# A selective-scan kernel on one core: the first column of `u B` made on GpSimd and copied in ahead of the product, Silu blocks opened for copies, and other buffers

## The chip, the cores and the metric

The kernel runs on one core of a Trainium2 chip. The metric is the device time of one execution in microseconds (us); less is better. Engine names are those of the profile: PE is TensorE's matmul, PEld its weight load, DVE is VectorE, ACT is ScalarE, POOL is GpSimd, SP is SyncE, which issues most DMAs.

## The reference, cut to what matters

The input has 4 images of 256 channels and 64 x 64 positions. Two mixers follow each other on every position, and then a layer of 8 experts with 1 choice per token. The change lies in the first mixer, a Mamba block with 512 inner channels and 16 states:

```
dt = softplus(dbl[..., :DT_RANK] @ dt_w.T + dt_b)
A = -exp(A_log)
def step(h, inp):
    dt_l, B_l, C_l, x_l = inp
    dA = exp(dt_l[..., None] * A)
    h = dA * h + (dt_l * x_l)[..., None] * B_l[:, None, :]
    y = einsum('bdn,bn->bd', h, C_l)
    return (h, y)
```

The second mixer (a state space block with 8 heads) is computed in matrix form, chunk by chunk, in `ssd`. All arithmetic is float32.

## The kernel before, in words

The program has three phases one after the other: `mixers`, `experts` and `turn`. The change touches only `mixers`, which takes the first five sixths of the time.

**Chunks and stages.** The positions of each image are cut into 16 chunks of `T` = 256, 64 chunks in all. A chunk goes through `front0` (projections and convolution of the first mixer), `mid0` (dt, and `u` = dt times x, written to DRAM), `scan`, `tail0`, `front1`, and two chunks later through `ssd` and `back1`. At any time, stages of several chunks are under way side by side.

**The scan.** `scan` works in 16 units per chunk: `j` (0 to 3) takes 128 of the 512 channels, `f` (0 to 3) takes four of the 16 states. Partitions hold 4 states times 32 channels, and a tile of a unit is [128, 4, 256]: four groups of channels, each with 256 positions. Per unit

- ACT makes the decay `da` (four exponentials of 255 columns; column 0 stays 0, so that four sequences can run through one scan);
- DVE makes `ub`, the product of `u4` and B (`bc[:, 0]`), into PSUM (one buffer);
- for a chunk that is not the first of its image, DVE adds `e0[:, :, f]`, four elements, to column 0 of `ub`: the state carried over from the chunk before times its decay. `e0` is made once per `j` for the four units: a product on POOL, an Exp on ACT, and a product with `hlast` of the chunk before on POOL;
- DVE runs `tensor_tensor_scan` over 1024 elements into `h`;
- ACT copies the last column of `h` to `hlast`;
- POOL makes `p`, the product of `h` and C (`bc[:, 1]`);
- PE sums `p` over states into `py`.

`bc4` tiles hold B and C of one `f`, are loaded from DRAM by SP at the start of each chunk and kept for all four `j`; there are five buffers. `gx` holds, for two `j` at a time, the pass-through input (used at `py`'s start by ACT) and the gate (used by DVE for `k_.g` at the end of the pair); there are two buffers of both together.

**What sets the order.** Nothing in `mixers` is emitted directly. Each operation is recorded by `Plan.note` with a weight (its planned cost in us), its tiles, and a slot: `k_.at(n)` gives it the place n, counted in units. `Plan.order` then plays the queues of the five engines forward: on each engine it starts, among the operations that are ready and have room in their buffer rings, the one with the lowest slot. `SIGNAL` and `BEHIND` are what it charges from the end of an operation to the start of one that depends on it, on another engine or on the same one. An operation with `port` may not run on DVE while one runs on POOL and the other way round; DVE operations with two inputs in SBUF have it, and all on POOL do. `p` has `ride`: it is started within 0.2 us of a scan's start on DVE, or after a wait of `PATIENCE`, 4 us, and `issue` ties it in the program to the DVE operation that stood before that scan (`behind`). Two operations on the same tile depend on each other only where their index boxes meet. The order found becomes the program's, and every engine runs its queue in order; the program's own waits are made separately, from the memory that instructions touch.

**Silus.** ACT computes Silu and Tanh from another table set than Exp and Ln. `silus` collects the Silu (and half-angle Tanh) of a chunk's `pre0`, or of `pre1` and `bcs`, and the load of the usual set after them, in one operation, so that nothing else comes between them on ACT.

All recorded operations carry the line of `issue` (L373) in the profile, so they are told apart by tiles.

Of the kernel before, what the change touches and what calls it, by code (L numbers as in the profile page):

```python
# [14 lines left out]
AF = mybir.ActivationFunctionType  # L15
ALU = mybir.AluOpType
# [4 lines left out]
P = 128  # L21
T = 256
# [4 lines left out]
KC = C // P  # L27
KD = DI // P
NST = 16
SQ = 4  # L30
# [14 lines left out]
AHEAD = 4  # L45
# [77 lines left out]
class Op:  # L123
    def __init__(self, seq, engine, slot, step):
        self.seq, self.engine, self.slot, self.step = seq, engine, slot, step
        self.calls, self.weight, self.lag = [], 0.0, 0.0
        self.port = self.scan = self.ride = False
        self.behind = self.issued = None
        self.deps, self.users, self.roots = set(), [], []
        self.start = self.end = None  # L130
# [6 lines left out]
class Plan:  # L137
# [4 lines left out]


    SIGNAL = {"DVE": 0.13, "ACT": 0.19, "PE": 0.21, "POOL": 0.12}
    BEHIND = {"DVE": 0.13, "ACT": 0.14, "PE": 0.0, "POOL": 0.13}
    LANES = 8
    SPARE = {}
    PATIENCE = 4.0
# [69 lines left out]
    def act(self, out, src, func, **kw):  # L218
        aps = sum(isinstance(v, Part) or hasattr(v, "ap") for v in kw.values())
        w = 0.06 + self.width(out) / 1130 + 0.09 * aps  # L220
        self.note("ACT", w, self.nc.scalar.activation, (out, src, func), kw, (out,), (src, *kw.values()))

    def copy(self, out, src):
        self.note("ACT", 0.05 + self.width(out) / 1200, self.nc.scalar.copy, (out, src), {}, (out,), (src,))

    def acts(self, weight, calls):

        key = object()
        for f, args, out, src in calls:
            self.note("ACT", weight, f, args, {}, (out,) if out is not None else (), (src,), join=key)  # L230

    def dve(self, name, *args, **kw):
        out, *rest = (*args, *kw.values())
# [41 lines left out]
    def order(self):  # L275
# [19 lines left out]
        lanes, landings = ("SP",), []  # L295
        done = 0
        scan = before = last = shared = None

        def room(op, now):
            for root in op.roots:  # L300
# [9 lines left out]
        while done < len(self.ops):  # L310
            if not events:
                left = [o for o in self.ops if o.start is None and not o.missing][:20]
                raise RuntimeError("no order: " + str([(o.engine, o.slot, [r.ring for r in o.roots]) for o in left]))
            now = heappop(events)
            while events and events[0] <= now:
                heappop(events)
            for e in engines:
                while waiting[e] and waiting[e][0][0] <= now:
                    _, _, op = heappop(waiting[e])
                    insort(could[e], (op.slot, op.seq, op))  # L320
                if free[e] > now or e in lanes and len(landings) >= self.LANES and landings[-self.LANES] > now:
                    continue
                for i, (_, _, op) in enumerate(could[e]):

                    if op.ride and not (scan and now - scan.start < 0.2) and now - op.ready < self.PATIENCE:
                        continue
                    if op.port and port["DVE" if e == "POOL" else "POOL"] > now:
                        continue
                    if room(op, now):
                        break  # L330
                else:
                    continue
                del could[e][i]
                for root in op.roots:
                    if not root.begun:
                        root.begun = True
                        rings[root.ring].append(root)
                op.start, op.end = now, now + op.weight + op.lag
                free[e] = now + op.weight
                heappush(events, free[e])  # L340
                if e in lanes:
                    landings.append(op.end)
                    heappush(events, op.end)
                if op.port:
                    port[e] = free[e]
# [38 lines left out]
def tile_conv_attn_hybrid(ctx: ExitStack, tc: tile.TileContext, a: dict, out: bass.AP, cap: int, st: int):  # L384
    nc = tc.nc
# [44 lines left out]
    def mixers(es):  # L430
# [29 lines left out]
        m_d = load("m_D")  # L460
# [85 lines left out]
        py = py_p.tile([P, 512], F32, name="py0", tag="py", bufs=1)  # L546
# [16 lines left out]
        SETS = "natural_log_exp_and_others"  # L563
# [3 lines left out]
        r = Plan(tc)  # L567

        def work(shape, tag, bufs=1):
            return r.tile(lambda: wk.tile(shape, F32, name=nm(tag), tag=tag, bufs=bufs), shape, tag, bufs)  # L570
# [86 lines left out]

        def silus(*tiles, gates=0):

            calls = [(nc.scalar.activation, (t, t, AF.Silu), t, t) for t in tiles]  # L660

            calls += [(half_tanh, (t[:, :KC],), t[:, :KC], t[:, :KC]) for t in tiles[:gates]]
            calls.append((nc.scalar.preload_act_table_set, (SETS,), None, None))
            r.acts(sum(0.06 + Plan.width(t) / 1130 for t in tiles) / len(calls) + 2.6 / len(calls), calls)

        def inv_sqrt(dst, src, eps, scale=1.0):

# [164 lines left out]
        for i in range(3):  # L832
            t = wp.tile([P, SQ, T], F32, name=f"da{i}", tag=f"da{i}")
# [7 lines left out]
        def scan(k_):  # L841
            later = k_.c > 0
            k_.hlast = work([P, NG, SQ], "hlast", 2)
            bc4 = []
            for f in range(SQ):

                k_.at(f - AHEAD)
                t = work([P, 2, T], "bc4", SQ + 1)
                for q in range(SQ):
                    r.dma("SP", t[q * R : (q + 1) * R], k_.bc_d[:, f * SQ + q].partition_broadcast(R))  # L850
                bc4.append(t)
            for j in range(KD):

                both = []
                for name, src in (("dt4", k_.dt_d), ("u4", k_.u_d)):
                    k_.at(j * SQ - AHEAD)
                    t = work([P, SQ, T], name, 2)
# [5 lines left out]
                dt4, u4 = both  # L863
                if j % 2 == 0:

                    gx = work([P, 2, 2, T], "gx", 2)
                    for s in range(2):
                        r.dma("SP", gx[:, s], k_.gx_d[s * KD + j : s * KD + j + 2].rearrange("j p l -> p j l"))
                sl = slice(j * SQ, (j + 1) * SQ)
                k_.at(j * SQ - 1)  # L870
                if later:

                    e0 = work([P, SQ, SQ], "e0", 2)
                    r.gps("tensor_tensor", e0, neg_a0[:, sl], dt4[:, :, 0:1].to_broadcast([P, SQ, SQ]), ALU.mult)
                    r.act(e0, e0, AF.Exp)
                    r.gps("tensor_tensor", e0, e0, k_.prev.hlast[:, sl], ALU.mult)
                for f in range(SQ):
                    u = j * SQ + f
                    bc = bc4[f]
# [3 lines left out]
                        r.act(da[:, q, 1:], dt4[:, q, 1:], AF.Exp, scale=neg_a0[:, j * SQ + q, f : f + 1])  # L883
                    k_.at(u)
                    ub = bank_u(SQ, T)
                    r.tt(ub, u4, bc[:, 0, None, :].to_broadcast([P, SQ, T]), ALU.mult)
                    if later:
                        r.tt(ub[:, :, 0], ub[:, :, 0], e0[:, :, f], ALU.add)
                    h = work([P, SQ, T], "h", 3)
                    r.dve("tensor_tensor_scan", h.flat(), da.flat(), ub.flat(), 0.0, ALU.mult, ALU.add)  # L890
                    k_.at(u + 1)
# [5 lines left out]
                    if f == 0:  # L897
                        if j % 2 == 0:
                            py = bank_y(2, T)
                            for i in range(2):  # L900
                                r.act(py[:, i], gx[:, 1, i], AF.Copy, scale=m_d[:, j + i : j + i + 1])
                    for i in range(SQ):
                        r.mm(
                            py[i * R : (i + 1) * R, j % 2],
# [7 lines left out]
                if j == 0:  # L912
                    k_.g = work([P, KD, T], "g0")
                if j % 2 == 1:
                    r.tt(k_.g[:, j - 1 : j + 1], gx[:, 0], py, ALU.mult)

# [24 lines left out]
        def front1(k_):  # L941
# [37 lines left out]
            for k in range(KC):  # L979
                for s in range(NS):  # L980
                    r.transpose(pt[:, k, s * Q : (s + 1) * Q], xn1[:, s, k * P : (k + 1) * P], ident)
            xn = work([P, KC, T], "t")
            r.copy(xn, pt)
            r.tt(ratio, ratio, scale[:, 1], ALU.mult)
            raw = work([P, KD, TAPS - 1 + T], "raw")
# [585 lines left out]
```

## Time and profile before

| | |
|---|---|
| time, median of 3 runs | 6704.4 us (6696.8 to 6706.3) |
| profiled execution | 6706.9 us, its span 6704.9 us |
| PE busy | 6188.0 us, 92% of the span |
| DVE busy | 5552.4 us, 83% |
| ACT busy | 4879.5 us, 73% |
| POOL busy | 3295.2 us, 49% |
| DMA | 1078 MB, 161 GB/s on average |
| granted clock of TensorE | 0.957 |

A line of a group of instructions gives the source line, the engine, the operation, the tiles (output `<-` inputs, buffer numbers left out), the shapes and the count; then the busy time in us and the mean of one in ns; then the engine's idle time just before these instructions, and what ended it. A line of a timeline gives start and length in us, engine, line, operation, tiles, and in brackets the idle time before it. Instructions of one engine can overlap in the records, since the next may start before the last one's end. A line of the waits gives who waited for whom, the total, the number of times and the longest. A line of the stretches gives the stretch, its length, then busy time and number of instructions of PE, PEld, DVE, ACT and POOL, the granted clock, the share of DMA and GB/s.

### The profile page before, as it was taken

To read this page: it belongs to the slowest core of one execution; us is meant where nothing else is said; L and a number is where in the kernel's file an instruction comes from. 1 tells how busy PE (TensorE), PEld (TensorE's weight loads), DVE (VectorE), ACT (ScalarE), POOL (GpSimd) and SP (SyncE) were. 2 spreads that over 40 slices of the span, in tenths; PEclk is the share of its full clock that TensorE was granted. 3 is DMA by queue.
4 is the path that set the end of the run, shared out by engine and by line. 5 is a ranking of instruction groups with operands and counts; after the bars stand their busy time and mean duration, and the time that the engine had idled before them with its cause. 6 is when DMAs were issued, how large, how long until landed. Compare 5 with 4: busy or idle time off the path is not lost. (4 is left out here: it accounts for less than half of the span.)

```text
span 6704.9 us, 111610 instructions
## 1 busy us (share of the span) xinstructions
PE 6188.0 (92%) x37578; PEld 4282.6 (64%) x37578; DVE 5552.4 (83%) x7685; ACT 4879.5 (73%) x11999; POOL 3295.2 (49%) x2622
## 2 busy tenths in 40 slices
PE   7899999999999999999999999999999977999997
PEld 5566666666666666666666666666666646888886
DVE  5999999999999999999999999999999983434443
ACT  5888888888888888888888888888888863333333
POOL 4655555555555555555555555555555552333331
PEclk8999999999999999999999999999999988999998
DMA  6854445455555545455545555555555434555556
GB/s 188 234 149 150 150 147 151 146 151 152 152 153 152 149 145 151 146 150 150 152 148 150 153 153 153 153 153 152 151 153 152 149 102 143 199 199 195 200 197 260
DMA packets 924401, 1078.46 MB, mean 161 GB/s; under 512 B 93537, under 2 KB 895077, under 8 KB 912435
## 3 DMA queue, kind: packets, MB, share of 16 engines
q1 hardware_dynamic: 890002, 842.27, 42.2%
q0 software_dynamic: 29472, 212.28, 8.7%
q10 hardware_dynamic: 4352, 16.78, 0.6%
q8 instruction: 296, 4.85, 0.3%
q14 instruction: 279, 2.28, 0.1%
HBM read 787.00 MB, written 276.76 MB: 159 GB/s over the span
## 5 line engine op out<-in xcount | busy, mean ns | idle before, releaser
L373 POOL TENSOR_TENSOR p<-h,bc 128x1024 f32<-128x1024 f32 x1024 | 2411.3, 2355 | 2008.0 <-DVE ub L373 507.2
L373 DVE TENSOR_TENSOR_SCAN h<-da,ub 128x1024 f32<-128x1024 f32 x1024 | 2339.5, 2285 | 78.1 <-ACT da L373 5.8
L373 ACT ACTIVATE da<-dt,w_m_Alog 128x255 f32<-128x255 f32 x4096 | 1842.6, 503 | 0.0
L373 DVE TENSOR_TENSOR ub<-u,bc 128x1024 f32<-128x1024 f32 x1024 | 1279.7, 1250 | 13.3 <-DMA u<-u_d 5.9
L373 PE MATMUL py<-p,sum 128*32 128x256 f32 x8192 | 662.4, 396 | 183.4 <-POOL p L373 176.8
L373 PE MATMUL b<-t,w_W_in 128*128 128x256 f32 x2304 | 579.6, 392 | 25.6 <-ACT bcs L373 4.9
L373 PEld LDWEIGHTS b<-t,w_W_in 128*128 128x128 f32 x2304 | 418.7, 190 | 189.9 <-ACT raw L373 76.2
L373 PE MATMUL a<-t,w_m_in_w 128*128 128x256 f32 x2048 | 511.3, 393 | 3.1 <-DVE t L373 2.8
L1411 PE MATMUL ph<-xt,w 128*128 128x256 f32 (+1 forms) x2304 | 496.1, 368 | 12.2 <-ACT hid L1413 11.9
L373 PEld LDWEIGHTS py<-p,sum 128*32 128x32 f32 x8192 | 168.9, 108 | 508.0 <-POOL p L373 259.2
L373 PE MATMUL a<-raw,taps_m 128*128 128x256 f32 x2048 | 480.6, 382 | 4.8 <-ACT pre L373 4.8
L1422 PE MATMUL po<-w,hid 128*128 128x256 f32 x2160 | 478.0, 379 | 0.0
L373 PEld LDWEIGHTS a<-t,w_m_in_w 128*128 128x128 f32 x2048 | 371.3, 191 | 145.1 <-issue 73.3
L373 PEld LDWEIGHTS a<-raw,taps_m 128*128 128x128 f32 x2048 | 377.4, 189 | 130.1 <-ACT e L373 39.0
L1411 PEld LDWEIGHTS ph<-xt,w 128*128 128x128 f32 x2304 | 412.3, 190 | 69.5 <-ACT hid L1413 17.9
L1422 PEld LDWEIGHTS po<-w,hid 128*128 128x128 f32 x2160 | 409.7, 190 | 55.3
L373 ACT COPY hlast<-h 128x4 f32<-128x4 f32 x1024 | 202.9, 198 | 278.7 <-DVE h L373 266.1
L1385 DVE CAST number<-rows 128x2 uint32<-128x2 f32 x72 | 12.3, 170 | 450.1 <-DMA tok_d<-fixed,number 437.7
L1383 ACT ACTIVATE tn<-rows 128x256 f32<-128x256 f32 x135 | 77.4, 596 | 401.0 <-DMA rows<-buf_d,row_at 400.3
L1434 POOL DMA_INDIRECT tok_d<-fixed,number x135 | 138.5, 1026 | 402.6 <-DVE fixed L1432 265.0
L373 PE MATMUL c<-cum,after 128*128 128x512 f32 x512 | 321.1, 713 | 14.5 <-ACT dend L373 13.7
L373 ACT ACT_TABLE_LOAD x256 | 328.4, 1283 | 4.7
(237 smaller groups left out, 11312.0 us busy)
## 6 DMA issues: line engine op xcount, KB each, us to landing
dt<-dt_d SPq DMA_DIRECT2D x1024, 128.0 KB, 2.5
u<-u_d SPq DMA_DIRECT2D x1024, 128.0 KB, 2.3
raw<-raw_d SPq DMA_DIRECT2D x1024, 128.0 KB, 3.3
gx_d<-pre SPq DMA_DIRECT2D x64, 1024.0 KB, 4.5
bc<-bc_d SPq DMA_DIRECT2D x1024, 64.0 KB, 2.5
gx<-gx_d SPq DMA_DIRECT2D x256, 256.0 KB, 3.1
raw_d<-raw SPq DMA_DIRECT2D x64, 518.0 KB
dt_d<-mid SPq DMA_DIRECT2D x64, 512.0 KB, 3.2
```

Source lines behind the costliest of these rows:

```text
L373: op.issued = f(*map(placed, args), **{k: placed(v) for k, v in kw.items()})
L1383: act(tn[:, j], rows[:, j, TOK:], AF.Identity, scale=rows[:, j, 1:2], bias=rows[:, j, 2:3])
L1385: nc.vector.tensor_copy(number, rows[:, :, 3])
L1411: mm(ph, w1[:, k, f * P : (f + 1) * P], xt[:, k], start=k == 0, stop=k == KC - 1)
L1422: mm(po[:, j], hid[:, f, j * P : (j + 1) * P], w2[:, f], start=f == 0, stop=f == KF - 1)
L1434: nc.gpsimd.indirect_dma_start(out=tok_d, out_offset=bass.IndirectOffsetOnAxis(ap=number[:, j : j + 1], axis=0), in_=fixed[:, j], in_offse ...
```

## The change

- `e0` of four units now also gets the first column of `u B`: ACT copies column 0 of each B tile to `b0`, POOL multiplies it with column 0 of `u4` (`u0`) and adds it to `e0`.
- DVE copies `e0[:, :, f]` to column 0 of `ub`, and the product fills only columns 1 to 255. The copy is recorded ahead of the product. The first chunk of an image keeps the full product.
- `silus` records its calls one by one. Between them the planner may place operations that every table set has (`copy`, and `act` with Identity or Copy); any other waits for the end of the set.
- `bc4` has six buffers for five. `gx` becomes `pass` and `gate`, one buffer each, loaded at slots of their own. `front1`'s `xn` gets a tile of its own, where it shared the ring `t`.
- The planner's charge from one DVE operation to one that depends on it becomes .17 for .13.

```diff
-    BEHIND = {"DVE": 0.13, "ACT": 0.14, "PE": 0.0, "POOL": 0.13}
+    BEHIND = {"DVE": .17, "ACT": 0.14, "PE": 0.0, "POOL": 0.13}
...
-    def acts(self, weight, calls):
-
-        key = object()
-        for f, args, out, src in calls:
-            self.note("ACT", weight, f, args, {}, (out,) if out is not None else (), (src,), join=key)
+        op.any_set = True
+
+    def acts(self, calls):
+
+        ops = []
+        for n, f, args, out, src in calls:
+            op = self.note("ACT", n, f, args, {}, (out,) if out is not None else (), (src,))
+            op.set = ops
+            if ops:
+                ops[0].deps |= op.deps
+                op.deps = {ops[-1]}
+            ops.append(op)
+        ops[0].deps -= set(ops)
...
                 for i, (_, _, op) in enumerate(could[e]):
+                    if e == "ACT" and in_set and not (op.any_set or op.set is in_set):
+                        continue
...
+                if op.set:
+                    in_set = op.set if op is not op.set[-1] else None
...
-            r.acts(sum(0.06 + Plan.width(t) / 1130 for t in tiles) / len(calls) + 2.6 / len(calls), calls)
+            load = 1.3
+            calls = [(weight(t), nc.scalar.activation, (t, t, AF.Silu), t, t) for t in tiles]
+            calls += [(weight(t[:, :KC]), half_tanh, (t[:, :KC],), t[:, :KC], t[:, :KC]) for t in tiles[:gates]]
+            calls[0] = (calls[0][0] + load, *calls[0][1:])
+            calls.append((load, nc.scalar.preload_act_table_set, (SETS,), None, None))
+            r.acts(calls)
...
-                t = work([P, 2, T], "bc4", SQ + 1)
+                t = work([P, 2, T], "bc4", SQ + 2)
...
+                if later:
+                    if f == 0:
+                        b0 = work([P, SQ], "b0", 2)
+                    r.copy(b0[:, f : f + 1], t[:, 0, :1])
...
-                    gx = work([P, 2, 2, T], "gx", 2)
-                    for s in range(2):
-                        r.dma("SP", gx[:, s], k_.gx_d[s * KD + j : s * KD + j + 2].rearrange("j p l -> p j l"))
+                    both = []
+                    for s, name, n in ((1, "pass", -AHEAD), (0, "gate", 3)):
+                        k_.at(j * SQ + n)
+                        t = work([P, 2, T], name)
+                        r.dma("SP", t, k_.gx_d[s * KD + j : s * KD + j + 2].rearrange("j p l -> p j l"))
+                        both.append(t)
+                    passed, gate = both
...
+                    u0 = work([P, SQ, SQ], "u0", 2)
+                    r.gps(
+                        "tensor_tensor",
+                        u0,
+                        b0[:, None].to_broadcast([P, SQ, SQ]),
+                        u4[:, :, 0:1].to_broadcast([P, SQ, SQ]),
+                        ALU.mult,
+                    )
+                    r.gps("tensor_tensor", e0, e0, u0, ALU.add)
...
-                    r.tt(ub, u4, bc[:, 0, None, :].to_broadcast([P, SQ, T]), ALU.mult)
+                    t0 = 0
                     if later:
-                        r.tt(ub[:, :, 0], ub[:, :, 0], e0[:, :, f], ALU.add)
+                        t0 = 1
+                        r.dve("tensor_copy", ub[:, :, 0], e0[:, :, f])
+                    r.tt(ub[:, :, t0:], u4[:, :, t0:], bc[:, 0, None, t0:].to_broadcast([P, SQ, T - t0]), ALU.mult)
...
-            xn = work([P, KC, T], "t")
+            xn = work([P, KC, T], "xn")
```

More of the change, by code (lines that the diff above doesn't have):

```diff
@@ L126, in __init__ @@
         self.calls, self.weight, self.lag = [], 0.0, 0.0
-        self.port = self.scan = self.ride = False
+        self.port = self.scan = self.ride = self.any_set = False
+        self.set = None
         self.behind = self.issued = None
@@ L220, in act @@
         w = 0.06 + self.width(out) / 1130 + 0.09 * aps
-        self.note("ACT", w, self.nc.scalar.activation, (out, src, func), kw, (out,), (src, *kw.values()))
+        op = self.note("ACT", w, self.nc.scalar.activation, (out, src, func), kw, (out,), (src, *kw.values()))
+        op.any_set = func in (AF.Identity, AF.Copy)
     def copy(self, out, src):
-        self.note("ACT", 0.05 + self.width(out) / 1200, self.nc.scalar.copy, (out, src), {}, (out,), (src,))
-    def acts(self, weight, calls):
-        key = object()
-        for f, args, out, src in calls:
-            self.note("ACT", weight, f, args, {}, (out,) if out is not None else (), (src,), join=key)
+        op = self.note("ACT", 0.05 + self.width(out) / 1200, self.nc.scalar.copy, (out, src), {}, (out,), (src,))
+        op.any_set = True
[9 more added lines that the diff above has]
+        ops[0].deps -= set(ops)
     def dve(self, name, *args, **kw):
@@ L297, in order @@
         scan = before = last = shared = None
+        in_set = None
         def room(op, now):
@@ L658, in silus, with weight @@
         def silus(*tiles, gates=0):
-            calls = [(nc.scalar.activation, (t, t, AF.Silu), t, t) for t in tiles]
-            calls += [(half_tanh, (t[:, :KC],), t[:, :KC], t[:, :KC]) for t in tiles[:gates]]
-            calls.append((nc.scalar.preload_act_table_set, (SETS,), None, None))
-            r.acts(sum(0.06 + Plan.width(t) / 1130 for t in tiles) / len(calls) + 2.6 / len(calls), calls)
+            def weight(t):
+                return 0.06 + Plan.width(t) / 1130
+            load = 1.3
[4 more added lines that the diff above has]
+            r.acts(calls)
         def inv_sqrt(dst, src, eps, scale=1.0):
@@ L900, in scan @@
                             for i in range(2):
-                                r.act(py[:, i], gx[:, 1, i], AF.Copy, scale=m_d[:, j + i : j + i + 1])
+                                r.act(py[:, i], passed[:, i], AF.Copy, scale=m_d[:, j + i : j + i + 1])
                     for i in range(SQ):
@@ L914, in scan @@
                 if j % 2 == 1:
-                    r.tt(k_.g[:, j - 1 : j + 1], gx[:, 0], py, ALU.mult)
+                    r.tt(k_.g[:, j - 1 : j + 1], gate, py, ALU.mult)
         def tail0(k_):
```

## The prediction

> **What bounds the kernel now.** I read the page first: busy shares and the 40 slices. The mixers (the planned phase with the scans) fill slices 1 to 33; only there does the change act. Then the sums over stretches inside that phase:
>
> ```profile
> 3000.00:4000.00 1000.00, 936.12 (x5966) 612.82 (x5964) 938.04 (x1261) 830.26 (x2072) 534.20 (x414) 0.97 0.51 151
> ```
>
> The first five counts are PE, PE loads, VectorE (DVE), ScalarE (ACT), GpSimd (POOL). DVE and PE are both near 94%, so DVE is first by a nose and PE is close behind: time freed on DVE meets PE soon. A chunk lasts 84.0 us (3001.47 to 3085.49 in DVE's timeline, from the `state` add behind one scan to the same add a chunk later).
>
> Next, the groups of instructions, by form, of DVE and POOL:
>
> ```profile
> L373 DVE TENSOR_TENSOR_SCAN h<-da,ub 128x1024 f32<-128x1024 f32 x1024 | 2339.5, 2285 | 78.1 <-ACT da L373 5.8 <-ACT mid L373 1.0 <-DVE red L373 0.8
> L373 DVE TENSOR_TENSOR ub<-u,bc 128x1024 f32<-128x1024 f32 x1024 | 1279.7, 1250 | 13.3 <-DMA u<-u_d 5.9 <-DVE ex L373 0.2
> L373 DVE TENSOR_TENSOR decay<-decay,gm 128x1024 f32<-128x1024 f32 x128 | 239.8, 1873 | 0.2
> L373 DVE TENSOR_TENSOR ub<-ub,e 128x4 f32<-128x4 f32 x960 | 159.4, 166 | 14.8 <-DVE ub L373 0.5
> L373 DVE TENSOR_TENSOR mid<-mid,mid 128x1024 f32<-128x1024 f32 x128 | 157.4, 1230 | 0.1
> L373 POOL TENSOR_TENSOR e<-e,hlast 128x16 f32<-128x16 f32 x240 | 107.5, 448 | 284.5 <-ACT e L373 284.4
> ```
>
> The fourth is the add that goes away, 960 times. The third takes 1873 ns where the same form takes 1230 (`mid`). The timelines of DVE and of POOL say why:
>
> ```profile
> 3043.15 1.30 DVE L373 TENSOR_TENSOR ub<-u,bc 128x1024 f32<-128x1024 f32 x1
> 3044.49 0.17 DVE L373 TENSOR_TENSOR ub<-ub,e 128x4 f32<-128x4 f32 x1
> 3044.79 2.29 DVE L373 TENSOR_TENSOR_SCAN h<-da,ub 128x1024 f32<-128x1024 f32 x1
> 3046.99 0.40 DVE L373 TENSOR_TENSOR state<-state,dend 128x256 f32<-128x256 f32 x1
> ...
> 3052.25 2.58 DVE L373 TENSOR_TENSOR decay<-decay,gm 128x1024 f32<-128x1024 f32 x1
> ```
>
> ```profile
> 3051.39 2.35 POOL L373 TENSOR_TENSOR p<-h,bc 128x1024 f32<-128x1024 f32 x1
> ```
>
> `decay` starts while `p` runs, and ends 1.1 us after it. The first three lines price dependence: the add starts 0.04 us after the product it waits for, the scan 0.13 after the add; the independent `state` starts 0.09 before the scan ends. So an instruction right behind what it waits for loses 0.12 us on DVE, a scan 0.22.
>
> Last, DVE's waits from 500 to 5300 us (total, times, longest):
>
> ```profile
> DVE cdec L373 <- ACT cdec L373: 75.1, 50, 3.4
> DVE stats L373 <- PE b L373: 70.6, 57, 3.9
> DVE xdt L373 <- PE c L373: 33.6, 108, 0.9
> DVE row L373 <- PE c L373: 28.0, 23, 1.3
> ```
>
> All its waits together are 236 us there.
>
> **What the skill says.** The Trainium skill, GPSIMD Engine Reference, § Key points: GpSimd shares its SBUF interfaces with VectorE and contends with two-SBUF-input instructions; the trace agrees (2.58 against 1.23). VectorE: DVE Perf Modes, § What auto-detection actually checks: the two-port copy mode needs source and destination in SBUF, so a copy into PSUM `ub` should not contend; no row shows that yet. ScalarE: Activation LUTs, § What ACT_TABLE_LOAD costs: 1283 ns each, and our 256 loads average 1283; § Table sets: copy and identity are in every set, so copies within a Silu set need no further load, and the built program indeed keeps its count of loads.
>
> **The change, part by part.**
>
> *Copy for add.* 960 adds become 960 copies. In the built program the copy does not run free: the product of the other 255 columns waits for it (the two regions interleave in `ub`), though the planner takes them as independent. I count neighbours on DVE in the order of both programs. Scans right behind what they wait for: 511 before, 229 after, at 0.215: 110 to 49 us. Scans with one small instruction between, which hides about 0.1: 294 to 210 at 0.12: 35 to 25. Products, adds and copies right behind what they wait for: 514 (207 products behind scans, 307 adds behind products) to 875 (608 products behind copies, 204 copies behind scans, the rest other pairs), at 0.12: 62 to 105. With one small between: 416 to 351 at 0.045: 19 to 16. Sum 226 to 195: **-30 us**. The copy itself: nearest rows are other tiny instructions of one input, 159 ns (RECIPROCAL) and 172 (CAST), against 166; I take 10 ns less, -10, ends -25 and +10. Four fewer elements of 1250 ns: 960 x 5 ns = -4. **Together -44**, ends -70 and 0.
>
> *Where `p` runs.* The new order is planned anew throughout, with DVE's dependence priced .17 for .13. Before, 178 of 1024 `p` are released a scan late, and about one per chunk lands on `decay`: 128 x (1873 - 1230) ns = 82 us. After, 953 of 1024 are released with a scan as DVE's next instruction (before 682), and only 3 a scan late. I take most of the collision as gone, **-75**, and of the excess of `ub` (1024 x 25 ns = 26 us) **-10**. Ends -108 and 0: it could return at another instruction if POOL runs late.
>
> *GpSimd's part.* Per four units two more instructions (`u0`, `e0 += u0`): 480. The rows of the same form take 409 and 448 ns, 0.22 alone in the timeline: 106 to 215 us on POOL, which is idle 47% of the stretch. They have two SBUF inputs each, so may hold up a DVE product: full collision would be 480 x 0.22 = 106. Of today's stretched DVE instructions some 6 us overlap `e`; I take **+6**, ends 0 and 106. Behind them on POOL stands `p`; 0.4 us lie inside its idle time, except where scans follow at 3.9 us with an output scatter (1.07 us): 2.35 + 1.07 + 3 x 0.22 = 4.1, late by 0.2.
>
> *ScalarE.* 240 copies of one column at about 0.2 us (`hlast`, 198 ns): 48 us, on an engine idle 17%: 0. Opened Silus let copies pass inside 5.6 us blocks, for PE's `raw` and `pre` evacuations a gain, but Exp (`da`, `decay`, `cdec`) waits longer for the set's end. `da` has three buffers, so a scan is covered; 0 here, the rest below.
>
> *Buffers and queues.* The sixth `bc4` frees the fourth tile of the next chunk a unit sooner, which `u0` needs. SP's transfers are as many (5197), only placed otherwise; the single `gate` and `pass` are reloaded with five units and more to spare. `xn` and `t` part. 0, ends -10 and +30.
>
> *Waits.* From `z` to `stats` DVE now has a scan more in between (some 8 us against 6 in the chunks I listed), and `cdec` stands behind the scan, not inside a unit before it. I take 50 of the 236 us as gone: **-50**, ends -140 and +100.
>
> Sum -44 -75 -10 +6 -50 = -173. PE's work stays: its own waits there are 279 us in all, 124 of them for `p`, 5.5 us a chunk. Taking 173 (2.7 a chunk) from that would leave half. I take three quarters of the sum, **-130**: the profiled execution's 6706.9 becomes 6577; its median, 6704.4, is 2.5 below it, within the run's spread.
>
> **The rivals.**
> 1. *Only the direct part counts.* DVE saves its 44 us but the collision moves to another product or PE holds the rest: -15 to -65, about 6660. For: PE at 94%. Against: 953 `p` next to a scan.
> 2. *Nothing.* DVE's freed time becomes waits on PE one for one: within 13 us of 6705. Against: much of PE's waiting is itself for `p` and DVE.
> 3. *Slower: the first column comes late.* The chain is the DMA of the fourth `bc` (released by `p` of the third unit from the end), ACT's copy, `u0`, the add, DVE's copy. ACT is in order, and that copy stands inside or near the Silu set with `da` behind it. Today POOL waits for `bc` 46 times, up to 3.0 us. From the point where `bc` lands later than the end of the chunk's last scan plus the some 4 us of `gm`, `xdt`, `decay`, `ub`, DVE stands; 3 us over in 60 chunks is 180, less 120 gained: +60, 6767. Against: landing takes 2.5 us and a unit 3.9 or more; the planner assumes over 3.5.
>
> **How the numbers follow.** Likeliest, the main case, 0.60: 6500 to 6640, at 6577. Rival 1 0.16, rival 2 0.06, rival 3 and other new stalls 0.18. Faster 0.76, the same (within 0.2%, 13 us, about what a measurement here can tell) 0.06, slower 0.18. The range goes from 6490 (the waits' far end, as much as PE's idle time lets through) to 6725, which leaves out the larger part of rival 3.
>
> **What would show it.** A mean of `decay` near 1.25 us; a copy row of 960 at 0.14 to 0.18 us, products 0.04 us behind it; `p` beginning with scans; a chunk of 81 to 82.5 us; PE busy 95 to 97%. I would be wrong if the copy's group showed idle time released by POOL `e`, if ACT's `b` showed waits for `bc`, or if DVE's waits for PE grew past 300 us.

## The result and the profile after

The kernel after takes 6661.8 us (median of 4 runs, 6656.6 to 6667.7), against 6705.4 for the kernel before in the same comparison: ratio 0.9945, 95% interval 0.993 to 0.996. It is faster by 44 us by the medians and by 37 us by the ratio, where 130 were forecast. The number lies in the forecast range, but outside the main case's 6500 to 6640.

In the kernel after, the line of `issue` is L387. First the stretch that was shown of before (PE, PE loads, DVE, ACT, POOL; granted clock, DMA share, GB/s):

```profile
3000.00:4000.00 1000.00, 930.87 (x5976) 625.91 (x5969) 927.66 (x1250) 833.73 (x2109) 607.83 (x500) 0.96 0.52 149
```

DVE and PE are both a little less busy than before (938 and 936); only POOL does clearly more (608 us for 534). A chunk takes 84.5 us on average (the ninth to the sixtieth of 64), where it took 85.4 (the one chunk read in the prediction, 84.0, was shorter than the average); 81 to 82.5 were forecast, and PE was to be busy 95 to 97%. The groups by form, of DVE and POOL:

```profile
L387 DVE TENSOR_TENSOR ub<-u,bc 128x1020 f32<-128x1020 f32 x960 | 1240.3, 1292 | 23.7 <-DMA raw<-raw_d 0.4
L387 DVE TENSOR_TENSOR decay<-decay,gm 128x1024 f32<-128x1024 f32 x128 | 159.7, 1248 | 0.3
L387 DVE COPY ub<-e 128x4 f32<-128x4 f32 x960 | 153.4, 160 | 34.7 <-POOL e L387 27.3
L387 POOL TENSOR_TENSOR u<-b,u 128x16 f32<-128x16 f32 x240 | 88.0, 369 | 102.4 <-ACT b L387 84.0 <-DMA u<-u_d 12.1 <-DMA dt<-dt_d 1.9
L387 POOL TENSOR_TENSOR e<-e,u 128x16 f32<-128x16 f32 x240 | 74.5, 310 | 10.3
L271 POOL DMA_INDIRECT buf_d<-row,dest x128 | 207.2, 1618 | 87.7 <-DVE dest L387 37.3 <-DMA u<-u_d 23.8 <-issue 10.2
```

`decay` has fallen from 1873 to 1248 ns and the 166 ns add has become a 160 ns copy, but the mean of `ub` has risen from 1250 to 1292 although it covers four elements less. The idle time ahead of the copy names POOL's `e`: the warning sign of the third rival, at 27 us and not 180. It was one of three signs of being wrong; the other two did not come: ACT's copies into `b0` show no wait for `bc`, and DVE's waits for PE rose from 157 to 217 us, not past 300. The last row is the output scatter on POOL, the indirect DMA that writes finished rows to `buf_d`; its issue took 1096 ns before. Timelines of DVE and of POOL (start, length) show where `ub` pays:

```profile
2503.57 2.28 DVE L387 TENSOR_TENSOR_SCAN h<-da,ub 128x1024 f32<-128x1024 f32 x1
2505.88 0.17 DVE L387 COPY ub<-e 128x4 f32<-128x4 f32 x1
2506.08 2.10 DVE L387 TENSOR_TENSOR ub<-u,bc 128x1020 f32<-128x1020 f32 x1
```

```profile
2503.60 1.08 POOL L271 DMA_INDIRECT buf_d<-row,dest  x1 [1.61 <-DVE dest L387]
2504.71 2.38 POOL L387 TENSOR_TENSOR p<-h,bc 128x1024 f32<-128x1024 f32 x1
```

`p` is planned to ride with the scan at 2503.57. The scatter stands ahead of it in POOL's queue and takes the first 1.1 us of that scan, so `p` outlasts the scan by 1.2 us and the next product takes 2.10 us for 1.23. The copy at 2505.88 also runs beside `p` and still takes 0.17 us: it does not contend, as the Trainium skill (VectorE: DVE Perf Modes, § What auto-detection actually checks) let one expect of a copy into PSUM. (In the whole trace the 372 copies that run beside a `p` take 166 ns in the mean and none over 175, the others 156.) Last, DVE's waits from 500 to 5300 us (total, times, longest), and the first row of PE's:

```profile
DVE pre L387 <- PE c L387: 50.4, 29, 2.3
DVE g L387 <- PE py L387: 47.3, 29, 2.1
DVE stats L387 <- PE b L387: 40.4, 39, 1.9
DVE gm L387 <- PE c L387: 31.4, 39, 1.3
DVE ub L387 <- POOL e L387: 24.2, 32, 1.1
```

```profile
PE py L387 <- POOL p L387: 182.3, 112, 4.6
```

Most of the names are new: `cdec` (75 us before) is gone and `xdt` has shrunk to 0.9, `pre` and `g` have come and `gm` has doubled, and the sum has not fallen (236 us before, 260 after). PE's waits for `p` were 126 us before.

**An account of DVE.** From the first scan's start to the last scan's end, every us of DVE is a record, minus the overlap of records, or a gap. Summed from the trace, gaps under 0.15 us apart from longer ones:

| | before | after | measured | forecast |
|---|---|---|---|---|
| `decay` | 239.8 | 159.7 | -80 | -75 |
| `ub` products | 1279.7 | 1323.0 | +43 | -14 |
| add or copy | 159.4 | 153.4 | -6 | -10 |
| other records | 3787 | 3783 | -4 | +6 (held up by POOL's new operations) |
| short gaps (dependence) | 97 | 69 | -28 | -30 |
| long gaps (waits) | 268 | 300 | +32 | -50 |
| overlap of records | -401 | -401 | 0 | |
| sum | 5430 | 5387 | -43 | -173 |

So `ub` took back half of what `decay` gave, and the waits did not shrink. The experiments ask why.

### The profile page after: what moved, and what is told of

The parts are those of the page before. It is cut to its first block, busy times and chain, and to the rows that moved or that the text cites. A ratio compares the mean times of both kernels' runs of the same rounds, so it can differ in the third digit from the quotient of the medians.

```text
span 6655.8 us, 112537 instructions
## 1 busy us (share of the span) xinstructions
PE 6129.7 (92%) x37578; PEld 4329.3 (65%) x37578; DVE 5507.6 (83%) x7685; ACT 4895.8 (74%) x12239; POOL 3670.0 (55%) x3102
## 5 line engine op out<-in xcount | busy, mean ns | idle before, releaser
L387 POOL TENSOR_TENSOR p<-h,bc 128x1024 f32<-128x1024 f32 x1024 | 2413.0, 2356 | 1477.0 <-DVE mid L387 189.8
L387 DVE TENSOR_TENSOR_SCAN h<-da,ub 128x1024 f32<-128x1024 f32 x1024 | 2336.7, 2282 | 38.1 <-ACT da L387 6.0
L387 ACT ACTIVATE da<-dt,w_m_Alog 128x255 f32<-128x255 f32 x4096 | 1815.9, 502 | 0.6
L387 DVE TENSOR_TENSOR ub<-u,bc 128x1020 f32<-128x1020 f32 (+1 forms) x1024 | 1323.0, 1292 | 31.4 <-DMA u<-u_d 6.8
L387 PE MATMUL py<-p,sum 128*32 128x256 f32 x8192 | 666.8, 398 | 246.4 <-POOL p L387 243.4
L387 PE MATMUL b<-xn,w_W_in 128*128 128x256 f32 x2304 | 570.5, 389 | 57.6 <-ACT raw L387 16.2
L387 PEld LDWEIGHTS b<-xn,w_W_in 128*128 128x128 f32 x2304 | 428.4, 191 | 177.3 <-ACT raw L387 61.0
L387 PEld LDWEIGHTS py<-p,sum 128*32 128x32 f32 x8192 | 175.4, 109 | 541.0 <-POOL p L387 318.3
L387 PE MATMUL a<-t,w_m_in_w 128*128 128x256 f32 x2048 | 509.4, 393 | 2.2 <-DVE t L387 1.9
L387 PE MATMUL a<-raw,taps_m 128*128 128x256 f32 x2048 | 490.6, 387 | 4.7 <-ACT pre L387 4.7
L387 PEld LDWEIGHTS a<-raw,taps_m 128*128 128x128 f32 x2048 | 376.4, 189 | 148.9 <-issue 92.5
L387 PEld LDWEIGHTS a<-t,w_m_in_w 128*128 128x128 f32 x2048 | 377.6, 192 | 122.6 <-issue 50.7
L387 ACT COPY hlast<-h 128x4 f32<-128x4 f32 x1024 | 200.5, 196 | 197.1 <-DVE h L387 194.5
L387 ACT ACTIVATE cum<-upto,da 128x128 f32<-128x128 f32 x1024 | 339.6, 399 | 0.7 <-DVE da L387 0.7
```

What stands on the lines that cost most here:

```text
L387: op.issued = f(*map(placed, args), **{k: placed(v) for k, v in kw.items()})
```

## The experiments

All ratios are to the kernel before in the same comparison. Long gaps, `decay` and `ub` are those of the account. Ratios are compared where kernels were measured in different comparisons, and 0.001 is 6.7 us.

### One edit at a time, planned anew

The edits are those of the diff above, taken or left whole: e1 is the kernel before with the first column alone, e2 the kernel after without it, e5 the kernel after with the Silus joined again, e6 the kernel after with the old buffers, e9 and e10 the kernel before with the new buffers or the opened Silus alone. e3, e15 and e16 change only this line in the kernel before, e9 and e10; e11 and e12 change it back, from .17 to .13, in e2 and in the kernel after:

```diff
-    BEHIND = {"DVE": 0.13, "ACT": 0.14, "PE": 0.0, "POOL": 0.13}
+    BEHIND = {"DVE": .17, "ACT": 0.14, "PE": 0.0, "POOL": 0.13}
```

> The kernel before with the first column alone (b0, u0, copy ahead of the product); buffers, Silus and the planner's charge as before. Theory A (the gain of the change is p released with scans, so that it no longer meets decay, and a part of it is given back where a scatter on POOL stands ahead of p): in this order 959 of 1024 p are released with a scan, so decay falls from 1873 to about 1250 ns (-80 us), dependent neighbours on DVE save 50 us, and ub grows above 1290 ns since 119 p stand right behind a scatter (+45): about 6630. Theory B (new plans scatter the time by some 40 us whatever the edit): anywhere from 6640 to 6720, with decay low or high. Theory C (PE holds the end): not under 6655, DVE's waits for PE over 250 us.

> The changed kernel without the first column: the add behind the product as before, the rest (Silus, buffers, charge .17) changed. Theory A: 905 p released with a scan, so decay is low here too (about 1250 to 1350 ns); the time is within 15 us of the changed kernel's 6662, and the column itself brings nothing but its own 6 us. Rival: the column is what brings the gain, and this one is within 15 us of the kernel before, 6705, with decay near 1870 ns.

> The kernel before with the planner's charge .17 for .13 and nothing else. Theory A: 821 p released with a scan (682 before) and 45 a scan late (178 before): decay halfway, some 1400 to 1600 ns (-35 to -60 us), dependent neighbours -48: about 6630 to 6660. Theory B: from 6640 to 6720. If it is at 6700 or more, the charge is not what moved p.

> The changed kernel with the Silus joined again in one operation (loads charged 2.6 together as before); column, buffers, .17 as changed. Theory D (what made the column alone 470 us slower is that with five bc4 the column of the next chunk's first unit comes too late for the plan, and the buffers cure it): within 40 us of the changed kernel's 6662, since the buffers are there. Theory E (the column's copies on ACT need the opened Silus): near 7100, DVE's waits for PE and ACT over 500 us.

> The changed kernel with the buffers of before: five bc4, gx in two buffers of both halves, xn in the ring t; column, opened Silus, .17 as changed. Theory D: slow, 6900 to 7200, chunks of about 90 us, as with the column alone. Theory E: within 40 us of 6662.

> The kernel before with the buffers alone (six bc4, single gate and pass, xn apart from t); no column, joined Silus, .13. In its order 869 of 1024 p ride with a scan (682 before) and 25 are a scan late (178 before). If the gain of the change comes from p having its product (bc) free sooner, this alone brings most of it: decay's mean falls from 1873 to about 1300 ns and the time to 6650-6680. If what is saved on decay turns up again as waits or on ub, the time stays within 15 us of 6705 although decay falls.

> The kernel before with the opened Silus alone; old buffers, no column, .13. In its order 686 of 1024 p ride and 165 are late, as before, so decay should stay near 1850 ns. If opened Silus shorten PE's evacuations (raw, pre) and with them DVE's waits for PE, the time falls by 20 to 50 us and the rows xdt, row and stats waiting for PE shrink. If they only help where the column's copies would be caught behind a block, the time stays within 13 us of 6705.

> Opened Silus and the buffers, no column, .13 (e2 without .17). If .17 matters for the waits (it alone cost 8 us on the kernel before), this is 5 to 15 us faster than e2's 6659: about 6648. If the two edits and not the charge make the gain, and a new plan merely scatters the time, it is within 15 us of 6659 on either side.

> The kernel after with the charge back at .13: column, opened Silus, buffers. In its order 892 p ride and 36 are late (953 and 3 after), 122 stand behind a scatter (99 after). If .17 is what keeps the column from costing, this is 6700 or more. If the charge does nothing here, it is within 15 us of 6662.

> e9 (the buffers alone) with the charge at .17. Same instructions, another order: 769 p ride, 129 are late (869 and 25 in e9). By the steps of the prediction (20 us fewer for neighbours, some 60 more for decay) it would be 40 us slower than e9: about 6645. If the new plan spreads the waits whatever these counts are, it can land anywhere from 6600 to 6700, and the difference will be in the long gaps and not in decay.

> e10 (opened Silus alone) with the charge at .17. Same instructions, another order: 881 p ride, 21 are late (686 and 165 in e10), and the loss at dependent neighbours is 184 us for 221. By the steps of the prediction it would be 100 us faster than e10: about 6540. If the plan spreads the waits, decay falls to about 1250 ns as counted and the time does not follow: 6600 to 6700.

| run | column, Silus, buffers | charge | us | ratio (interval) | `decay` + `ub`, us | long gaps, us |
|---|---|---|---|---|---|---|
| before | none | .13 | 6705 | 1 | 240 + 1280 | 268 |
| e3 | none | .17 | 6712.7 | 1.0028 (1.002 to 1.0035) | 179 + 1355 | 290 |
| e10 | Silus | .13 | 6638.9 | 0.9924 (0.9905 to 0.9942) | 245 + 1280 | 210 |
| e16 | Silus | .17 | 6801.6 | 1.014 (1.0123 to 1.0157) | 156 + 1370 | 360 |
| e9 | buffers | .13 | 6605.4 | 0.9868 (0.9852 to 0.9885) | 159 + 1347 | 145 |
| e15 | buffers | .17 | 6797.6 | 1.0134 (1.0117 to 1.0151) | 161 + 1387 | 297 |
| e11 | Silus, buffers | .13 | 6696.3 | 1.0 (0.9991 to 1.0009) | 158 + 1358 | 297 |
| e2 | Silus, buffers | .17 | 6659.0 | 0.9944 (0.9927 to 0.996) | 162 + 1292 | 287 |
| e1 | column | .13 | 7167.1 | 1.0699 (1.0672 to 1.0726) | 158 + 1345 | 754 |
| e5 | column, buffers | .17 | 6827.1 | 1.0187 (1.0165 to 1.0209) | 156 + 1328 | 399 |
| e6 | column, Silus | .17 | 6934.6 | 1.0331 (1.0311 to 1.035) | 156 + 1339 | 538 |
| e12 | all | .13 | 6660.0 | 0.9948 (0.9931 to 0.9965) | 159 + 1313 | 306 |
| after | all | .17 | 6661.8 | 0.9945 (0.993 to 0.996) | 160 + 1323 | 300 |

e5, e9, e11, e15 and e16 came out outside every range that their expectations gave, and e1 agrees only with "not under 6655". Three things follow.

**The edits do not add up.** By the ratios, the buffers alone bring 88 us, which makes e9 the fastest kernel of those that leave nothing out, faster than before and after. The Silus alone bring 51. Both together bring nothing at .13 and 38 at .17, and the column on top of both brings nothing at .17 (e2 against after) and 35 at .13 (e11 against e12). The column alone costs 469.

**The charge, which changes no work at all, moves the time as far as the edits**: from e9 to e15 by +0.0266, some 178 us, from e10 to e16 by some 145, and from e12 to after by nothing (on the kernel before, e3, it costs 19). The counts that my forecast rested on do not foretell this: by them e16, with fewer dependent neighbours and 881 `p` riding, should have been 100 us faster than e10. DVE's waits (total, times, longest) in e9, and then in e15, which runs the same operations:

```profile
DVE gm L373 <- PE c L373: 54.4, 40, 2.3
DVE xdt L373 <- PE c L373: 20.9, 77, 0.3
DVE cdec L373 <- ACT cdec L373: 19.8, 19, 1.1
DVE row L373 <- PE c L373: 11.6, 48, 0.5
DVE stats L373 <- PE b L373: 5.0, 6, 1.7
```

```profile
DVE state L373 <- PE c L373: 96.3, 56, 2.6
DVE gm L373 <- PE c L373: 59.9, 55, 2.5
DVE stats L373 <- PE b L373: 52.2, 26, 3.3
```

The `state` and `stats` rows, 56 times 1.7 us and 26 times 2.0, are places in the order where an operation of DVE stands before PE's result is there.

**The collision moves.** In every new order but e10's `decay` runs free or nearly so (least so in e3, at 1.40 us in the mean), and in nearly all of them `ub` has grown: `decay` + `ub` is 1519 us before, 1483 after, 1506 in e9, 1548 in e15. e3 already showed it: `decay` -61, `ub` +75.

In e1 the third rival's mechanism can be looked for directly. DVE's waits there:

```profile
DVE gm L373 <- PE c L373: 144.7, 49, 3.5
DVE xdt L373 <- PE c L373: 127.2, 92, 3.4
DVE g L373 <- PE py L373: 92.2, 86, 1.3
...
DVE ub L373 <- POOL e L373: 26.7, 40, 3.0
```

The column's own wait, the last row, is 27 us of the 469 that e1 loses. Most of the rest stands at operations that do not read it and wait for PE; whether the late column is what delays PE there was not tested. e5 (+125 us) and e6 (+222) say that, at .17, it takes both the opened Silus and the buffers to plan the column without a loss; why the planner's order is so bad without them was not settled.

### The scatter moved behind the next `p`

The order of the kernel after, with each output scatter emitted behind the `p` that follows it:

```diff
...
-        for op in self.order():
+        ops = self.order()
+        for op in [o for o in ops if o.scatter]:
+            i = ops.index(op)
+            n = next((k for k in range(i + 1, len(ops)) if ops[k].engine == "POOL"), None)
+            if n is not None and ops[n].ride:
+                ops.insert(n, ops.pop(i))
+        for op in ops:
```

> The changed kernel, with its plan as it is, except that a scatter that stands right ahead of a p in POOL's order is emitted behind that p. Theory A: the products of units 13 to 15 are no longer stretched: ub's mean falls from 1292 to about 1250 ns (-40 us on DVE), p starts with its scan there; 6662 becomes 6620 to 6640. Theory C: DVE's waits for PE grow by as much, and the time stays within 10 us of 6662.

6659.9 us, 0.9942 (0.9919 to 0.9964), as the kernel after. `ub` falls by 23 us, as it should if the scatter ahead of `p` stretches it, and the long gaps rise by 14, from 299.9 to 313.5. The cause of the excess is confirmed at its place: in unit 14 of a chunk it falls from 32.5 to 0.5 us in all, while in unit 15, where another scatter stands, it rises from 13 to 21. Its removal is worth nothing in this order. (By the trace of the kernel after, products lose 67 us in all over 1.232 us each: 47 beside a `p` that starts right behind a scatter, 17 beside one right behind the first product of `e0`, which the kernel before has too.)

### Is it PE's work, or the length of `p`?

Both kernels in their own orders, with one of the four taps of the convolution left on PE (e7, e8: the other three are missing from the result):

```diff
+                f, args, kw = r.ops[-1].calls[0]
+                r.ops[-1].calls = [(f, args, {"start": True, "stop": True})]
                 r.act(dst, pi, AF.Identity, bias=bias[:, j : j + 1])
```

> The kernel before with its plan as it is, where each convolution of the first mixer issues one of its four taps, so its output leaves three out: about 368 us less on PE (3/4 of 491), nothing less on DVE. Theory C (PE holds what DVE gains): PE is the near bound, so this one is faster too, by 40 to 150 us. Theory F (DVE and POOL hold, PE follows): within 20 us of 6700, PE's waits grow by the 368.

> The changed kernel with its plan as it is, with one of four taps as in the other run. Theory C: the difference between the changed kernel and before, 43 us with full PE work, grows to 80 to 150 us when PE is relieved, and DVE's waits for PE (230 us) fall below 120. Theory F: the difference stays 30 to 55.

6724.7 us, 1.0023 (1.0009 to 1.0037), and 6674.0 us, 0.9942 (0.9923 to 0.9961). The stretch from 1000 to 5000 us, of e7 and of e8:

```profile
1000.00:5000.00 4000.00, 3563.86 (x22635) 2258.35 (x22631) 3701.58 (x4962) 3298.81 (x8212) 2110.22 (x1615) 0.95 0.51 151
1000.00:5000.00 4000.00, 3614.26 (x22895) 2361.33 (x22893) 3724.59 (x5005) 3346.85 (x8475) 2402.87 (x1982) 0.92 0.53 152
```

There PE is busy 3751 us in the kernel before and 3740 in the kernel after. It now does less, and neither kernel gains. PE's amount of work is not what took the forecast gain. (The granted clock fell too, from 0.957 to 0.942 and from 0.953 to 0.918, and the matmuls of `py` got longer, from 396 to 403 ns and from 398 to 426, so a part of the relief was lost; PE's busy time is lower all the same.)

Then, again in their own orders, with `p` computed over half of its columns and PE reading that half twice:

```diff
                     r.gps("tensor_tensor", p, h, bc[:, 1, None, :].to_broadcast([P, SQ, T]), ALU.mult, ride=True)
+                    if True:
+                        g_, a_, kw_ = r.ops[-1].calls[0]
+                        r.ops[-1].calls = [(g_, (p[:, :2], h[:, :2], bc[:, 1, None, :].to_broadcast([P, 2, T]), ALU.mult), kw_)]
...
+                        g_, a_, kw_ = r.ops[-1].calls[-1]
+                        r.ops[-1].calls[-1] = (g_, (a_[0], a_[1], p[:, i % 2]), kw_)
```

> The kernel before in its own order, with p computed for the first half of its columns only and PE reading that half twice (half of the scans' outputs is left out of y). p falls from 2.35 to about 1.2 us, PE's work is the same. If DVE's waits are there because p comes late to PE's queue (chain scan, p, py, c or b, DVE), PE's 126 us for p fall below 40 and DVE's waits fall by 100 or more: below 6550 with the collisions of p gone too (decay -80, ub -20). If p is not what sets the waits, only the collisions go: 6610 to 6650.

> The kernel after in its own order, with the same half p (half of the scans' outputs is left out of y). The excess of ub in units 13 to 15 (some 65 us) goes. If p's lateness also sets DVE's waits for PE (pre, g, gm, stats), PE's 182 us for p fall below 60 and the time to 6500 or less. If the waits stay (300 us of long gaps), only the excess goes: 6590 to 6620.

On the kernel before: 6499.8 us, 0.9694 (0.9678 to 0.971), 205 us less. On the kernel after: 6626.6 us, 0.9883 (0.9866 to 0.9899), 42 us less than after. In the account, e13's records shrink by 151 us and its long gaps from 268 to 226: most of its gain is shorter records of DVE (`decay` and `ub` 107 of the 151), and about a fifth is waits. e14's records shrink by 107 us, and its long gaps grow from 300 to 363. The stretch of e13 from 1000 to 5000 us, and DVE's waits of e14:

```profile
1000.00:5000.00 4000.00, 3823.22 (x24779) 2523.28 (x24778) 3760.13 (x5176) 3432.60 (x8583) 1248.97 (x1690) 0.99 0.53 157
```

```profile
DVE g L387 <- PE py L387: 76.0, 30, 6.2
DVE gm L387 <- PE c L387: 68.4, 57, 1.9
DVE stats L387 <- PE b L387: 57.2, 39, 3.5
DVE ub L387 <- POOL e L387: 31.8, 36, 1.4
```

PE can be busy for 3823 us of 4000, 96%, with this work and these dependences, so before and after (3751 and 3740) it had room. And what bounds the order of the kernel after is not `p`'s length either: PE's waits for `p` fall from 182 to 97 us, and DVE's for PE rise.

### The column's own work, with the order held still

Every edit so far also made a new order. e17 and e18 keep that of the kernel after. An operation whose calls are emptied keeps its place in the plan and issues nothing. e17 leaves out POOL's two new operations (the first column's `u B` is missing from every scan behind the first chunk); e18 also turns the copy and the shorter product back into the full product and the add:

```diff
...
+                    r.ops[-1].calls = []        # e17, e18: behind u0 and behind e0 += u0
...
+                        r.ops[-1].calls = []    # e18: behind the copy
                     r.tt(ub[:, :, t0:], ...)
+                        g_ = r.ops[-1].calls[0][0]
+                        r.ops[-1].calls = [
+                            (g_, (ub, u4, bc[:, 0, None, :].to_broadcast([P, SQ, T]), ALU.mult), {}),
+                            (g_, (ub[:, :, 0], ub[:, :, 0], e0[:, :, f], ALU.add), {}),
+                        ]
```

> The kernel after in its own order, with GpSimd's two new operations (u0 and e0 += u0) left out in their places (so the first column of u B is missing from every scan behind the first chunk). The prediction put them at 6 us. If that is right: 6650 to 6660. If DVE's 24 us of waits for e and the products that these operations stretch are real losses, 6620 to 6640. If the order's own waits swallow it, nothing: 6662.

> e17's program with the copy left out too, the product made over all columns again and the old add right behind it: the old work in the order of the kernel after. By the prediction's working (add 6 us longer in all by the traces, 20 us more for dependent neighbours in this order, 4 elements more a product) it is 25 to 35 us slower than e17. If what DVE saves turns into waits for PE in this order, e17 and e18 agree within 10 us and the long gaps differ instead.

e17: 6625.6 us, 0.9889 (0.9872 to 0.9906). e18: 6762.9 us, 1.0086 (1.0072 to 1.0099). The way from before to after can now be walked in ratios: the order of the kernel after with the old column costs 58 us (e18), the copy in place of the add gains 132 (e18 to e17), and POOL's two operations cost 38 (e17 to after). The sum is -36, as after stands in these ratios; it has to, as the steps share their ends. By the intervals of the ratios, each step is known to some 15 us either way. DVE's groups of the copy in e17 and of the add in e18:

```profile
L388 DVE COPY ub<-e 128x4 f32<-128x4 f32 x960 | 153.7, 160 | 9.8 <-DVE ub L388 0.5
```

```profile
L388 DVE TENSOR_TENSOR ub<-ub,e 128x4 f32<-128x4 f32 x960 | 163.6, 170 | 34.4
```

The account from e17 to e18: records +24, overlap 25 less, short gaps +9, together 59 us of DVE; the long gaps rise by 85, from 243 to 327. So in this order 59 us more on DVE came with 85 more of waits, and cost 143. (The add stands right behind its product all 960 times here, and 307 times in the order of the kernel before, so the old work has its worst place.) From e17 to after the long gaps rise by 57, of which 24 are the waits for `e`. e17 lies in the second of its three ranges, where the waits for `e` are a real loss, so the prediction's 6 us fail; e18 lies outside both of its own.

## Why the prediction was right and wrong, by its steps

**Right.** *The direction, and why DVE spends less.* The collision with `decay` was the largest thing in the profile that the change removes, and it went (-80 for -75): 56 of 128 `decay` ran beside a `p` for half of their length or more before, none after. It is not owed to the column, as new orders without it removed it too (e2, e9, e16). The count of dependent neighbours held (-28 for -30), and so did POOL's busy time for the new operations (88.0 + 74.5 = 162 us, between 106 and 215). That the direction came out right owes something to luck: by the same steps e16 was to be 100 us faster than e10, and it was 145 slower.

**Wrong, the waits (-50, measured +32).** This is the largest miss. I named two waits, 146 us together, that the new order would shorten, credited 50 of them, and put new waits at nothing. They did shrink, by 105 us: `cdec` is gone from DVE's waits, and `stats` fell from 70.6 to 40.4. But the order is a new one everywhere, `pre` and `g` came, and `gm` doubled: all waits together went from 236 to 260, so the new ones brought some 129. The long gaps lie between 145 and 360 us in the orders without the column and between 300 and 754 with it, and a charge of .17 for .13 moves them from 145 to 297 with the same work. A term for waits in a replanned order has no value that two chunks of its listing could give; +32 lies within that spread.

**Wrong, the collision on `ub` (-10, measured +43 with the four fewer elements).** I counted `p` released with a scan and took the collision as gone. Released is not started: where an output scatter stands ahead of it, `p` starts 1.1 us into the scan and meets the next product. The prediction had worked out this very case for POOL's small operations ("late by 0.2") and not for the scatter itself, by counting 953 releases and no starts. In the trace of the kernel after, 785 of 1024 `p` start within 0.3 us of a scan's start (658 before). e4 shows the cause for the 23 us that it takes away; the rest of the excess is placed by the trace alone.

**Wrong, POOL's part (+6, measured 38 by e17).** I priced only products stretched by 0.22 us, and that part is not there: `ub` takes 1323 us with and without the two operations. The waits for `e` (24 us), listed under the third rival, belong here. e17 takes away 33 us more of long gaps; that each small operation holds up `p` and what follows would explain them, but no run places them.

**Wrong reason, three quarters for PE.** e7 and e8 took PE's work away without gain, e13 ran PE at 96%. No discount for PE's amount of work was due; it made the number smaller for a reason that these runs do not show. DVE did wait for PE 60 us more than before, but relieving PE did not shorten DVE's waits (long gaps of 322 us in e8, 300 in the kernel after). (PE's own waits, 279 us over 4700, are 5.1 us a chunk and not 5.5.)

**The rivals.** The first had the number (about 6660) and half the mechanism, so its hit is in part luck: the collision did move to another product, PE's load did not hold the rest. "Nothing" is excluded by the interval. The third had the right place, waits for `e`, at a seventh of its price; in e1 the loss was larger than the rival's and stood elsewhere.

**Not settled.** What sets the waits in the order of the kernel after. It is not PE's work alone (e8), nor `p`'s length alone (e14), nor the scatter (e4). No run loosened the tie of `p` to a scan: in the kernel after `p` starts 3.1 us behind the end of its own scan in the mean, and `p` is what PE waits for most, so this tie remains an untested candidate. The orders differ everywhere at once, so no single queue position is shown to be the cause.

## What to carry to other kernels

Where an edit makes a planner find a new order, forecast the removed work and the new work from the profile, but give the waits a width taken from replans of the same work (here some 180 us, four times the gain), and measure each edit also with the order held still. A count of releases says when an instruction may start: look at what stands ahead of it in its own queue before crediting a collision as gone. And try the parts of a bundle alone: here one of them beat the whole by 50 us.

## What was not expected of the hardware

Taking PE work away lowered the clock that it was granted: with three quarters of one convolution's matmuls gone it fell from 0.957 to 0.942 and from 0.953 to 0.918, and the mean of `py`'s matmul rose from 398 to 426 ns in e8. Among the kernels with all of PE's work, the fastest had the highest clocks and the slowest the lowest (0.974 at 6500 us, 0.970 at 6605, 0.920 at 7167), though not in strict order (0.946 at 6696, 0.952 at 6798). No run separates whether a low clock is a result of waiting or a cause of the time.

POOL's small operations have no fixed price. The same 16-element form of `e` takes 0.22 us alone and up to 1.30 us where a two-input product of DVE runs beside it, and the scatter's issue goes from 1.08 to 1.81 us:

```profile
2507.25 1.81 POOL L271 DMA_INDIRECT buf_d<-row,dest  x1 [0.17 <-issue]
2509.09 2.37 POOL L387 TENSOR_TENSOR p<-h,bc 128x1024 f32<-128x1024 f32 x1
2511.40 1.21 POOL L387 TENSOR_TENSOR e<-w_m_Alog,dt 128x16 f32<-128x16 f32 x1
```

Here the contention runs the other way from the one that the prediction looked for: DVE's products at 2506.08 and 2510.81 (1.74 us) hold up POOL as well. (Lengths on POOL are rough, but the starts agree: the next instructions start at 2509.09 and 2512.57.)
